# A decoder layer on one core: the feed-forward's first product as seven half-size products, its weight sums in a ring, and turned probabilities moved by half pairs

## Chip, cores and metric

The kernel runs on one core of a Trainium2 chip. The metric is the device time of one execution in microseconds. TensorE (PE) multiplies matrices, VectorE (DVE) and ScalarE (ACT) work element by element, GpSimd (POOL) does so too, and SyncE (SP) issues most of the DMAs. Each engine executes its instructions in the order in which the built program holds them.

## The reference

One decoder layer over 8 x 512 positions of width 512, with a layer norm behind each of its three parts. In the kernel `t` (0 to 7) is the first index and `j` a block of 128 of the 512 positions.

```python
x = layernorm(x + self_attn(x))          # 16 heads, over the 8 indices t, relative offsets
x = layernorm(x + cross_attn(ctx, x))    # 8 heads, 512 keys from a 512 x 1024 context, masked
x = layernorm(x + ffn(x))                # 512 -> 2048 -> 512

def ffn(x):
    h = relu(x @ w1.T + b1)              # float32
    hq = float_quantize(h, 4, 3)         # fp8
    return float_quantize(hq @ float_quantize(w2, 4, 3).T + bq, 5, 10)
```

The first product of `ffn` is, for each t, a 2048 x 512 matrix (w1) times a 512 x 512 matrix (x turned), in float32. It is what the change rewrites.

## The kernel before

The program has two phases.

**Phase 1** (to about 860 us) is the self-attention for each block j and, between its steps, the projection of the context into keys and values. For three pairs of t that projection is already done with seven half-size products in place of eight: sums of the weights (`sums_of_a`) and of the two contexts (`sums_of_b`) are formed on DVE, and each block of the result is a combination of a few products. The context sums stand in tiles `tx` (pool `tcp`, 4 buffers), read by the products `px` and `pz` (L662). A pacing planner written by hand (`must`, `fill`, `slot`) sets PE's order; the other engines' order in phase 1 is left to the scheduler. At the end of a block, `put_out` (from L346) multiplies the attention output by the output weights into the single bank of the pool `a_o`, loads the rows of x (`r`, L355, by SP), adds the bias to them on POOL (L356), adds the product on DVE (L362), and after every fourth t normalizes and stores the result to `x1d` (ACT's queue). In the last block, `put_out` for t = 4 to 7 is followed on PE by the context values of t = 6 (`psv`, L176).

**Phase 2** (from about 860 us) takes t = 0 to 7 in turn. All engines but POOL run in the order in which the steps are recorded. A function `weave` mixes two lists by their costs: the attention of t (scores `s`, weighted values `av`) and the "dense" steps. The dense steps of loop t are, in order: the output projection of t-1 (`project_x1`, `project_u`), its layer norm, the second feed-forward product of t-2 (`finish`, tile `o`), the queries of t+1 (`psq`, L1015), and the first feed-forward product of t-1 (`hidden`, tile `h`, L1229). Work on DVE, ACT and the queues that hangs on a step is put in lists (`urgent`, `side`, `moves`, `later`) and drained between the PE steps at a set pace.

- `hidden(t, n)` makes 128 of the 2048 rows at a time: four matmuls of 128 x 128 weights with the 512 positions of `x2T` moving, into one bank, then one ACT operation that adds the bias, applies relu and writes fp8 into `hq`. All of w1 (4 MB) lies in the buffer `big`, loaded once at t = 1.
- `x2T` is the layer norm's output in turned blocks: it is stored to `x2d`, loaded back in four DMAs (`load_blocks`, L937) and turned in place on DVE (`turn_x2`, L943), which stands between the queries 1 and 2 of the loop.
- The probabilities of one pair of heads, for a unit of half the queries (`jj` 0 or 1), are made by DVE and ACT in `scores`, turned in 32 x 32 blocks into `pb` (L1087), and, when both halves are there, moved across partitions into `pT` by 16 DMAs of 128 KB (`move_blocks`, L1102). All go to SP, but half of them to ACT's queue at t = 0. `pT` has one buffer, so the moves wait until `av` of the pair before has read it.
- At the end (after t = 7), `h` of the last t runs with nothing beside it but the second product of t = 6 and 7.

Of the kernel before, what the change touches and what calls it, by code (L numbers as in the profile page):

```python
# [17 lines left out]
P = 128  # L18
E = 512
# [23 lines left out]
def decoder_layer(  # L43
# [36 lines left out]
    def col(i):  # L80
        return colv[:, i : i + 1]
# [6 lines left out]
    x2d = [dram.tile([NJ, P, E], F32, name=f"x2d{t}") for t in range(T)]  # L88
    kd = [dram.tile([P, EC, S], F32, name=f"kd{t}") for t in range(T)]
    vd = [dram.tile([P, ST, E], F32, name=f"vd{t}") for t in range(T)]  # L90

    def load_row(pool, r, name):
        tl = pool.tile([P, E], F32, name=name)
# [38 lines left out]

    A11, A12, A22, S3, S1, S2, S4 = range(7)

    def sums_of_a(eng, w):
        eng.tensor_tensor(w[:, S1], w[:, S3], w[:, A22], ALU.add)
# [52 lines left out]
    with ExitStack() as ph:  # L191
# [570 lines left out]
        def last_but_one():  # L762
# [4 lines left out]
                T - 2, w6, lambda f: ct6[f], ps_kv, "kv", kst, "st"  # L767
            )

        filling.append(context_work())  # L770
        for j in range(NJ):
            for t in range(T) if j else range(2, T):
                if j and t == 0:
                    spare += [(FULL, values, j, u) for u in range(T)]
                items = []
                if t < T - 1:
                    items.append((FULL, queries_of, j, t + 1))


                if t < 4:  # L780
                    late = [t] if j or t > 2 else [0, 1, 2]
                else:
                    late = [[], [4, 5], [6], [7]][t - 4]
                items += [(0.9, offsets, j, u) for u in late]
                if j and t < 2:
                    items.insert(0, (0.9, turn_out, j - 1, T - 2 + t))
                if j and t < 3:
                    items.append((FULL, put_out, j - 1, T - 3 + t))
                slot(SCORES if j else SCORES + 1.9, items, T - 1 - t)
            softmax(j)  # L790
            last = j == NJ - 1
            if last:
                load_w6_keys()
                pieces = last_but_one()

                def values_in_turn():
                    load_w6_values()
                    yield -14.0
                    for piece in pieces[EC:]:
                        piece()  # L800
                        yield 2 * FULL

                filling.append(values_in_turn())
            else:
                spare += [(FULL, keys, j + 1, u) for u in range(T)]
            fill(clock + FULL)
            slot(SOFTMAX, [], max(len(spare) - 2, 0))
            for t in range(T):
                weigh(j, t)
                items = []  # L810
                if t > 1:
                    items.append((0.9, turn_out, j, t - 2))
                if t == T - 1:
                    if not last:
                        items.append((FULL, queries_of, j + 1, 0))
                if t > 2:
                    items.append((FULL, put_out, j, t - 3))
                if last and t == 0:
                    spare += [(2 * FULL, piece) for piece in pieces[:EC]]
                slot(VALUES, items, len(spare) if last else max(T - 3 - t, 0))  # L820
        for t in (T - 2, T - 1):
            must(0.9, turn_out, j, t)
# [25 lines left out]
    with ExitStack() as ph:  # L848
# [8 lines left out]
        mp = pool("mp", 1)  # L857
        kvd = pool("kvd", 2)
        sp = pool("sp", 7)
        pbp = pool("pb", 2)  # L860
        ptp = pool("ptp", 1)
        sm = pool("smb", 4)
        ps_b = pool("b_b", 4, space=PSUM)
# [50 lines left out]
        x1, x1T, qT, uT, mb, mvb, kT, v, pb, pT, x2T, hq, mvc = ({} for _ in range(13))  # L914

        def load(t):
            mbc = mp.tile([P, S], F32, tag="mbc", name=f"mbc{t}")
            nc.sync.dma_start(mbc, mask[t].partition_broadcast(P))


            mq = mp.tile([P, S], F32, tag="mq", name=f"mq{t}")
            nc.gpsimd.tensor_scalar(mq, mbc, -1.0 / math.sqrt(D2), None, ALU.mult)
            mb[t] = mp.tile([P, S], F32, tag="mb", bufs=2, name=f"mb{t}")
            nc.gpsimd.tensor_scalar(mb[t], mbc, 0.0, MASKED, ALU.is_equal, ALU.mult)
            qT[t] = qx.tile([P, EC, S], F32, tag="qT", bufs=2, name=f"qTx{t}")
            return mq

        def load_x1(t):
# [29 lines left out]
        def turn_x2(t):  # L958
            for c in range(EC):
                turn_in_place(x2T[t], c)  # L960

        def load_k(t, c):
            kT[t, c] = kvd.tile([P, S], F32, tag="kT", name=f"kT{t}_{c}")
# [48 lines left out]
        def queries(t, o, mq):  # L1012
            ps = bank(f"psq{t}_{o}")
            for e in range(EC):
                nc.tensor.matmul(  # L1015
                    ps,
                    lhsT=w_tgt[:, e, o * P : (o + 1) * P],
                    rhs=x1T[t][:, e, :],
                    start=(e == 0),
                    stop=(e == EC - 1),  # L1020
                )
            nc.vector.scalar_tensor_tensor(
                qT[t][:, o, :], ps, col(C_BT + o), mq, ALU.add, ALU.mult
            )

        def scores(t, c, jj):
# [4 lines left out]
            for j in js:  # L1031

                ps = ps_s.tile([P, 2, S], F32, tag="s", name=f"s{t}_{c}_{j}")
                for h in range(2):
                    nc.tensor.matmul(  # L1035
                        ps[:, h, :],
                        lhsT=qT[t][half[h], c, j * P : (j + 1) * P],
                        rhs=kT[t, c][half[h], :],
                        start=True,
                        stop=True,  # L1040
# [38 lines left out]
            def turn_blocks(i):  # L1079


                if i == 0 and jj == 0:
                    pb[t, c] = pbp.tile(
                        [P, 4, 2, ST, 2, 2, 32], F32, tag="pb", name=f"pb{t}_{c}"
                    )
                for h in range(2):
                    nc.vector.transpose(  # L1087
                        pb[t, c][:, :, jj, :, h, i, :].rearrange("p a k e -> p k a e"),
                        prs[2 * i + h].rearrange("p (k a e) -> p k a e", a=4, e=32),
                    )  # L1090

            def move_blocks():

                pT[t, c] = ptp.tile(
                    [P, 4, 2, ST, 2, 64], F32, tag="pT", name=f"pT{t}_{c}"
                )
                for i in range(4):
                    for a in range(4):
                        g = (a + i) % 4

                        queue = nc.scalar if t == 0 and a % 2 else nc.sync
                        queue.dma_start(  # L1102
                            pT[t, c][32 * a : 32 * a + 32, g],
                            pb[t, c][32 * g : 32 * g + 32, a].rearrange(
                                "p i k h j e -> p i k h (j e)"
                            ),
                        )

# [10 lines left out]
                side.append((u, 1.2, lambda i=i: divide(i)))  # L1119
            for i in range(2):  # L1120
                side.append((u, 1.3, lambda i=i: turn_blocks(i)))
            if jj == 1:
                side.append((u, 0.0, lambda: moves.append((u // 2, move_blocks))))

        def attend(t, c):

# [78 lines left out]
        def turn_last_x2(j):  # L1205
            t = T - 1
            if j == 0:
                settle(("x2", t))
                x2T[t] = qx.tile([P, EC, S], F32, tag="x2T", name=f"x2T{t}")
            turn(x2T[t], x1[t], j, f"x2tr{t}")  # L1210

        w1 = []

        def load_w1():

            w1.append(big.tile([P, EC, HID], F32, tag="big", name="w1"))
            for q in range(4):
                qs = slice(q * E, (q + 1) * E)
                nc.sync.dma_start(w1[0][:, :, qs], chunked(w1T)[:, :, qs])

        def hidden(t, n):

            if n == 0:

                tag, bufs = ("qT", 2) if t == T - 1 else ("hq", 1)
                hq[t] = qx.tile([P, HC, S], F8, tag=tag, bufs=bufs, name=f"hq{t}")
            ps = bank(f"h{t}_{n}")
            for e in range(EC):
                nc.tensor.matmul(  # L1229
                    ps,  # L1230
                    lhsT=w1[0][:, e, n * P : (n + 1) * P],
                    rhs=x2T[t][:, e, :],
                    start=(e == 0),
                    stop=(e == EC - 1),
                )
            nc.scalar.activation(  # L1236
                hq[t][:, n, :], ps, AF.Relu, bias=col(C_B1 + n), saturate=False
            )

        def finish(t, j, n):  # L1240

# [118 lines left out]
        with tc.manual_schedule(engines={ET.PE, ET.DVE, ET.Activation, ET.SP}):  # L1360
# [22 lines left out]
            scores(*units[0])  # L1383
            turn_v_soon(0)

            for t in range(T):

                pace = 1.3 if t == 0 else 0.7
# [29 lines left out]
                else:  # L1418
                    done = [of(3.8, finish, t - 2, j, NJ) for j in range(NJ) if t > 1]
                    if t == 1:  # L1420

                        done = [of(7.2, pieces[-2]), of(7.2, pieces[-1]), [], []]
                    dense += output_of(t - 1)
                    if t == 1:
                        dense[1:1] = of(0.0, convert, 2)
                    projected = len(dense)
# [10 lines left out]
                    if t == 1:  # L1437
                        dense += of(0.0, convert, 3)
                    if t == 1:
                        dense += of(0.0, load_w1)  # L1440
                    dense += done[2]
                    if t + 1 < T:
                        dense += of(0.0, turn_x1, t + 1)
                    dense += done[3]
                    dense += asked[:2] + of(0.0, turn_x2, t - 1) + asked[2:]
                    queried = len(dense)
                    for n in range(HC):
                        dense += of(3.6, hidden, t - 1, n)
                        if n == HC // 4:
                            dense += of(0.0, load_x1, t)  # L1450
                weave(dense, attention_of(t, projected, queried))

            last = of(3.8, finish, T - 2, 0, NJ) + output_of(T - 1)
            last += of(0.0, normalize_x2, T - 1)
            for j in (1, 2):
                last += of(3.8, finish, T - 2, j, NJ)
            for j in range(NJ):
                last += of(0.6, turn_last_x2, j)
            last += of(3.8, finish, T - 2, 3, NJ)
            for n in range(HC):  # L1460
                last += of(3.6, hidden, T - 1, n)
            for j in range(NJ):
                last += of(3.8, finish, T - 1, j, 1)
            for cost, step in last:
# [90 lines left out]
```

## Time and profile before

| | |
|---|---|
| runs | 2096.81, 2097.76, 2099.65 us; median 2097.76 |
| profiled execution | span 2097.7 us (its own time within 0.1 us of the median), granted PE clock 0.991 |
| PE busy | 2049.0 us (98%), 5768 records |
| DVE busy | 1432.4 us (68%) |
| ACT, POOL busy | 466.3 us (22%), 167.2 us (8%) |
| DMA | 255.27 MB, 122 GB/s mean |
| `h`, all of it | 451.8 us busy in 1024 records |
| moves `pT` from `pb` | 480 on SP's queue and 32 on ACT's, 128.0 KB each |

The profile is one execution, taken on the chip. A group of instructions is shown as line, engine, operation, output and inputs, shape and number, then its busy time, the mean duration of one, the engine's idle time just before them, and what ended that idle time. A float32 matmul leaves two records on PE. Matmuls are pipelined, so the mean duration of one is longer than the time from one start to the next. In a timeline a row is the start, the length, and the instructions that ran in it, with the idle time before in brackets. SPq rows are DMA issues: their length is what SP spends on issuing.

### The profile page before, as it was taken

Reading aid. Unit: us, or ns where it says so; the run is one execution under the profiler, and the core shown is the slowest. Engines: PE = TensorE matmul, PEld = TensorE weight load, DVE = VectorE, ACT = ScalarE, POOL = GpSimd, SP = SyncE. Lnnn points to the kernel's source line nnn. Section 1 sums busy time; section 2 is a strip of 40 time slices with the busy share of each in tenths; the row PEclk is TensorE's granted clock in tenths of the full one; section 3 lists DMA queues with packets and bytes.
Section 4 is the critical chain, followed back from the end, with each engine's and each line's share of the span. In section 5 each row is a group of like instructions: output and inputs, shape, how many; then the busy total and the mean of one; then the engine's idle time right before and its main releaser. Section 6 shows DMA issues by size and latency. Waiting matters only on the chain.

```text
span 2097.7 us, 17237 instructions
## 1 busy us (share of the span) xinstructions
PE 2049.0 (98%) x5768; PEld 889.9 (42%) x5768; DVE 1432.4 (68%) x2285; ACT 466.3 (22%) x955; POOL 167.2 (8%) x147
## 2 busy tenths in 40 slices
PE   9999999998999989998999999999999999999998
PEld 4544444444444434443443444444444434443443
DVE  4999999999899968367554754835747548357232
ACT  2111101110111101123232232231332322323211
POOL 0110120011001200121001011010010100001000
PEclk9999999999999989999999999999999999999999
DMA  6615333341131332885782744745636537437200
GB/s 217 225 40 201 106 105 131 110 155 65 57 144 60 137 149 70 260 222 139 160 214 67 133 118 101 136 116 93 139 84 110 141 87 146 100 80 152 53 21 20
DMA packets 246249, 255.27 MB, mean 122 GB/s; under 512 B 141072, under 2 KB 161552, under 8 KB 246160
## 3 DMA queue, kind: packets, MB, share of 16 engines
q1 hardware_dynamic: 227248, 219.25, 40.9%
q10 hardware_dynamic: 18912, 34.91, 5.0%
q8 instruction: 46, 0.75, 0.1%
q14 instruction: 43, 0.35, 0.1%
HBM read 130.36 MB, written 56.62 MB: 89 GB/s over the span
## 4 chain that ended last, share of the span: by engine, by line
PE 82%; DVE 13%; DMA 2%; issue 2%; SPq 0%; POOL 0%; ACT 0%; DVEq 0%; ACTq 0%
PE h L1229 21%; PE px L662 6%; PE s L1035 6%; PE pox L1174 5%; PE av L1137 5%; PE pox L1162 5%; PE psq L1015 5%; PE ps_k L216 5%; PE o L1246 4%; DVE pq L249 4%; DVE sc L258 3%; PE pz L662 3%; PE po L346 3%; PE psk L162 3%; PE psv L176 3%; PE ps_v L216 2%
## 5 line engine op out<-in xcount | busy, mean ns | idle before, releaser
L1229 PE MATMUL h<-x2T,w 128*128 128x512 f32 x1024 | 451.8, 596 | 2.3 <-DVE x2T L943 2.3
L1050 DVE CUSTOM_DVE_ANT_0 pe<-s,mb 128x512 f32<-128x512 f32 x256 | 162.1, 682 | 211.0 <-PE s L1035 211.0
L1229 PEld LDWEIGHTS h<-x2T,w 128*128 128x128 f32 x1024 | 191.1, 190 | 259.4 <-issue 254.2
L1060 ACT ACTIVATE pe<-pe,nmax 128x512 f32<-128x512 f32 x256 | 182.2, 712 | 209.1 <-DVE nmax L1050 178.9
L1087 DVE STREAM_TRANSPOSE pb<-pe 128x512 f32<-128x512 f32 x256 | 159.6, 679 | 0.0
L1236 ACT ACTIVATE hq<-h,colv 128x512 fp8e4<-128x512 f32 x128 | 87.9, 687 | 293.7 <-PE h L1229 293.7
L249 DVE TENSOR_TENSOR pq<-qw,k 128x2048 f32<-128x2048 f32 x64 | 151.1, 2361 | 1.1
L313 DVE TENSOR_TENSOR pv<-v,sc 128x2048 f32<-128x2048 f32 x64 | 146.5, 2290 | 1.9
L258 DVE TENSOR_REDUCE sc<-pq 128x64 f32<-128x2048 f32 x64 | 145.9, 2280 | 1.1
L1035 PE MATMUL s<-kT,qTx 64*128 64x512 f32 x512 | 127.2, 615 | 0.0
L216 PE MATMUL ps_k<-w_in,xt 128*128 128x512 f32 x256 | 118.0, 613 | 9.1 <-DMA xt<-in_xT_dram 4.9
L1137 PE MATMUL av<-pT,vx 128*64 128x512 f32 x512 | 118.5, 605 | 7.4 <-DMA mbc<-in_mask_dram 7.4
L216 PE MATMUL ps_v<-w_in,xt 128*128 128x512 f32 x256 | 116.4, 599 | 5.7 <-DVE qw L245 5.7
L346 PE MATMUL po<-w_o,aoT 128*128 128x512 f32 x256 | 115.5, 594 | 3.2 <-DVE r L362 3.2
L1075 DVE TENSOR_SCALAR pe<-pe,rden 128x512 f32<-128x512 f32 x256 | 114.9, 491 | 4.5
L216 PE MATMUL ps_q<-w_in,xt 128*128 128x512 f32 x256 | 116.0, 596 | 0.5 <-ACT v L286 0.3
L1174 PE MATMUL pox<-w_xo,uT 128*128 128x512 f32 x256 | 115.2, 598 | 0.0
L1162 PE MATMUL pox<-w_xo,x1Ts 128*128 128x512 f32 x256 | 114.4, 595 | 0.0
L1246 PE MATMUL o<-w2q,hq 128*128 128x512 fp8e4 x512 | 114.1, 379 | 0.0
L1015 PE MATMUL psq<-x1Ts,w_tgt 128*128 128x512 f32 x256 | 113.8, 597 | 0.0
L356 POOL TENSOR_TENSOR r<-r,bo 128x512 f32<-128x512 f32 x32 | 55.5, 1764 | 520.5 <-DMA r<-in_x_dram 323.9
L1181 DVE TENSOR_TENSOR x<-pox,x 128x512 f32<-128x512 f32 x32 | 22.1, 692 | 104.2 <-PE pox L1174 66.3
(142 smaller groups left out, 2150.1 us busy)
## 6 DMA issues: line engine op xcount, KB each, us to landing
pT<-pb SPq DMA_DIRECT2D x480, 128.0 KB, 2.4
ch<-in_ctxT_dram SPq DMA_DIRECT2D x24, 512.0 KB, 6.6
td<-tx SPq DMA_DIRECT2D x12, 768.0 KB, 4.8
tx<-td SPq DMA_DIRECT2D x12, 768.0 KB, 9.1
r<-in_x_dram SPq DMA_DIRECT2D x32, 256.0 KB, 3.4
x1d<-r ACTq DMA_DIRECT2D x32, 256.0 KB, 2.5
x1Ts<-x1d SPq DMA_DIRECT2D x32, 256.0 KB, 6.1
kT<-kd SPq DMA_DIRECT2D x32, 256.0 KB, 3.3
```

Of the source, the lines that this page charges most:

```text
L216: nc.tensor.matmul(ps, lhsT=xt[:, e, :], rhs=w_in[:, e, part * E : (part + 1) * E], start=(e == 0), stop=(e == EC - 1),)
L249: nc.vector.tensor_tensor(pr, qw[:, fs] .rearrange("p (h d) -> p h d", d=D1) .unsqueeze(2) .to_broadcast([P, HH, T, D1]), k_all[j][:, :, f ...
L258: nc.vector.tensor_reduce(sc[j][:, t, g * HH * T : (g + 1) * HH * T], pr.rearrange("p h s d -> p (h s) d"), AX.X, ALU.add,)
L662: nc.tensor.matmul(bank, lhsT=w7[:, a, f, i * P : (i + 1) * P], rhs=b[f], start=start and f == 0, stop=f == HF - 1, skip_group_check=not s ...
L1015: nc.tensor.matmul(ps, lhsT=w_tgt[:, e, o * P : (o + 1) * P], rhs=x1T[t][:, e, :], start=(e == 0), stop=(e == EC - 1),)
L1035: nc.tensor.matmul(ps[:, h, :], lhsT=qT[t][half[h], c, j * P : (j + 1) * P], rhs=kT[t, c][half[h], :], start=True, stop=True,)
L1060: nc.scalar.activation(pe, pe, AF.Exp, bias=nmax[:, h : h + 1], scale=-1.0, accum_out=den[:, h : h + 1],)
L1137: nc.tensor.matmul(av[half[h], :], lhsT=v[t, c][:, s, half[h]], rhs=pT[t, c][:, :, :, s, h].rearrange("p g i q -> p (g i) q"), start=(s == 0),
L1162: nc.tensor.matmul(po, lhsT=x1T[t][:, e, j * P : (j + 1) * P], rhs=w_xo[:, e, :], start=(e == 0), stop=False,)
L1174: nc.tensor.matmul(po, lhsT=uT[t][:, e, j * P : (j + 1) * P], rhs=w_xo[:, EC + e, :], start=False, stop=(e == EC - 1),)
L1229: nc.tensor.matmul(ps, lhsT=w1[0][:, e, n * P : (n + 1) * P], rhs=x2T[t][:, e, :], start=(e == 0), stop=(e == EC - 1),)
L1246: nc.tensor.matmul(po, lhsT=hq[t][:, c, j * P : (j + 1) * P], rhs=w2q[:, c, :], start=(c == 0), stop=(c == HC - 1),)
```

## The change

1. `hidden` is replaced by `hidden_of`. For each t the 2048 x 512 weights are taken as four groups, each of two halves of the rows (128 x 2 of the first half of the outputs, 128 x 2 of the second) and two halves of the contraction; the 512 positions are split in two halves of 256. A group needs seven products (`y`, `x1_`, `z`, `x2_`, `z2`, `x3`, `x4`) of four matmuls with 256 positions moving. Three of their results are copied with the bias by ACT (`keep`), three are added by DVE from PSUM (`add`) with a relu on ACT behind, and `x4` goes straight to relu. The last `x4` of a t is recorded in the next loop, behind its first `project_x1`.
2. The position sums: `sum_x2` records four additions on DVE behind the turn of `x2T`, between the queries 2 and 3.
3. The weight sums: `sum_w1` is recorded in the last eight slots of phase 1, twice in each. It takes a tile from `tx`'s buffers, loads four 128 x 128 blocks of w1, makes four additions on POOL and stores 7 x 128 columns to DRAM (`w1d`).
4. The weights, now 7/4 as large, don't stay: `big` holds a ring of two groups. Part 0 of a slot (three weights) is loaded again after `z`, part 1 (four weights) after `x4`, for the group after next.
5. `move_blocks` moves each half pair when it is turned: 16 DMAs of 64 KB per unit. `pb` has three buffers of a half pair in place of two of a pair.
6. The mask is loaded into its own tile `mq` without a tile `mbc`; the queries `qT` are four tiles per t with seven buffers; `hq` always has its own tag.

```diff
-    A11, A12, A22, S3, S1, S2, S4 = range(7)
+    A12, A11, S1, S2, S4, S3, A22 = range(7)
...
+        def sum_w1(n, f):
+            w = tcp.tile([P, 7, P], F32, tag="tx", name=f"w1s{n}_{f}")
+            for a, r, k in ((A11, 0, 0), (A12, 0, 1), (S3, 1, 0), (A22, 1, 1)):
+                o0 = r * (HID // 2) + n * P
+                nc.sync.dma_start(w[:, a], chunked(w1T)[:, 2 * k + f, o0 : o0 + P])
+            sums_of_a(nc.gpsimd, w)
+            nc.sync.dma_start(w1d[n // 2][:, :, f, (n % 2) * P : (n % 2 + 1) * P], w)
...
                     items.append((FULL, put_out, j, t - 3))
...
+                if last:
+                    for f in range(2):
+                        sum_w1(t, f)
                 slot(VALUES, items, len(spare) if last else max(T - 3 - t, 0))
...
+        def sum_x2(t):
+            b = blocks_of_x2(t)
+            x2s[t] = qx.tile([P, 3, 2, HALF], F32, tag="x2s", name=f"x2s{t}")
+            sums_of_b(
+                nc.vector,
+                b[0, 0],
+                b[0, 1],
+                b[1, 0],
+                b[1, 1],
+                *(x2s[t][:, i] for i in range(3)),
+            )
...
-            if jj == 1:
-                side.append((u, 0.0, lambda: moves.append((u // 2, move_blocks))))
+            side.append((u, 0.0, lambda: moves.append((u // 2, move_blocks))))
...
+            ps = slice(0, 3) if part == 0 else slice(3, 7)
+            nc.sync.dma_start(ring[0][:, q % 2, ps], w1d[q % GROUPS][:, ps])
...
+            def product(g, name, a, b, start):
+                w = ring[0][:, (t * GROUPS + g) % 2, a]
+                if start:
+                    banks[g, name] = bank(f"h{name}{t}_{g}").rearrange(
+                        "p (i q) -> p i q", i=2
+                    )
+                for f in range(2):
+                    for i in range(2):
+                        nc.tensor.matmul(
+                            banks[g, name][:, i],
+                            lhsT=w[:, f, i * P : (i + 1) * P],
+                            rhs=b[:, f],
+                            start=start and f + i == 0,
+                            stop=f == 1,
+                            skip_group_check=not (start and i == 0),
+                        )
+                return banks[g, name]
...
+            def keep(r, c, g, src):
+                st = kept[g, r, c] = hp.tile(
+                    [P, 2, HALF], F32, tag="hs", name=f"hs{t}_{g}_{r}{c}"
+                )
+                for i in range(2):
+                    nc.scalar.activation(
+                        st[:, i], src[:, i], AF.Identity, bias=bias(r, g, i)
+                    )
+
+            def add(r, c, g, src):
+                st = kept[g, r, c]
+                nc.vector.tensor_tensor(st, src, st, ALU.add)
+                nc.scalar.activation(target(r, c, g), st, AF.Relu, saturate=False)
...
+            def again(g, part):
+                later.append([1, lambda: load_w1(t * GROUPS + g + 2, part)])
...
+            def y(g):
+                start_of(g)
+                keep(0, 0, g, product(g, "y", A12, b(1, 0), True))
+
+            def x1_(g):
+                add(0, 0, g, product(g, "x", A11, b(0, 0), True))
+
+            def z(g):
+                keep(1, 1, g, product(g, "z", S1, x2s[t][:, 0], True))
+                again(g, 0)
+
+            def x2_(g):
+                keep(0, 1, g, product(g, "x", S2, x2s[t][:, 1], False))
+
+            def z2(g):
+                add(0, 1, g, product(g, "z", S4, b(1, 1), False))
+
+            def x3(g):
+                add(1, 1, g, product(g, "x", S3, b(0, 1), False))
...
+            order = [(y, 0), (x1_, 0), (z, 0)]
+            for g in range(GROUPS):
+                more = g + 1 < GROUPS
+                order += [(x2_, g), (z2, g)]
+                order += [(y, g + 1)] if more else []
+                order += [(x3, g)]
+                order += [(x1_, g + 1), (z, g + 1)] if more else []
+                order += [(x4, g)]
+            steps = [(1.8, lambda f=f, g=g: f(g)) for f, g in order]
+            return steps[:-1], steps[-1:]
...
-                    dense += asked[:2] + of(0.0, turn_x2, t - 1) + asked[2:]
+                    dense += asked[:2] + of(0.0, turn_x2, t - 1) + asked[2:3]
+                    dense += of(0.0, sum_x2, t - 1) + asked[3:]
```

## The prediction

> **What bounds the kernel now.** I read the busy table and the chain of waits first, then the groups, then the timelines of the stretches that the diff touches. The profiled execution's span is 2097.7 us; the median of the runs is 2097.76, so sums are made against 2097.7 and need no correction. Differences under 0.2% (4 us) count as no change.
>
> ```profile
> PE 2049.0 (98%) x5768; PEld 889.9 (42%) x5768; DVE 1432.4 (68%) x2285; ACT 466.3 (22%) x955; POOL 167.2 (8%) x147
> ...
> PE 82%; DVE 13%; DMA 2%; issue 2%; SPq 0%; POOL 0%; ACT 0%; DVEq 0%; ACTq 0%
> ...
> L1229 PE MATMUL h<-x2T,w 128*128 128x512 f32 x1024 | 451.8, 596 | 2.3 <-DVE x2T L943 2.3
> ```
>
> PE is the bound: 98% busy, 82% of the chain. A stretch with PE full, 1000 to 1900, has DVE at 524 of 900 us. The feed-forward's first product h is the largest PE group and waits only 2.3 us in all. An f32 matmul leaves two records, so its 512 instructions are x1024. Whatever makes PE wait is therefore added one for one, and whatever PE no longer does is gained one for one.
>
> **1. Fewer products: gain.** The chain of waits has the last position's h alone: 54.93 us for 128 records, 429 ns each. The new records are 128x256, which the trace lacks; the nearest are the bias products of phase 1, 128x128, 8 records in 1.05 us of a pipelined end, 16 in 1.95.
>
> ```profile
> 2022.38 54.93 PE h L1229 x128
> ```
>
> ```profile
> 648.59 1.05 PE L270 MATMUL bd<-gp,xt 128*128 128x128 f32 x8
> ...
> 700.90 1.95 PE L270 MATMUL bd<-gp,xt 128*128 128x128 f32 x16
> ```
>
> ```profile
> L270 PEld LDWEIGHTS bd<-gp,xt 128*128 128x128 f32 x256 | 33.5, 194 | 12.7 <-issue 12.7
> ```
>
> (1.95-1.05)/8 = 112 ns from start to start, with a new weight tile for every matmul, so weight loads of 194 ns overlap one another and don't bind at 112. A straight line between 112 (N=128) and 429 (N=512) gives 218 at N=256; ends are 214.5 (half of 429) and 224 (two of 112). New records: 8 positions x 4 groups x 7 products x 4 matmuls x 2 = 1792. 1792 x 0.218 = 390 against 1024 x 0.429 = 439: **-49 us** (-38 to -55).
>
> A rule speaks against this. The Trainium skill, "TensorE: Matmul & The Clock Gate", section "Back-to-back issue gap", says that in a stream with a weight load for every matmul the spacing is set by both, about 81 ns at N=128 where streaming alone gives 56. With 25 ns more per pass, by estimate from that page, a record would be some 268 ns and the change would lose 41 us here. Twice that page's unpenalised 56 is the 112 ns above, measured with weights that change every time, so this trace doesn't show the penalty.
>
> **2. Sums of the weights between the phases: loss.** The sums are recorded with the last slots of phase 1, but their tiles share the four buffers of the context sums tx, last read by the px products at 842.49. In the order of the built program, SP has r's load for put_out 4, then nearly all of the 64 loads of 64 KB and the 16 stores, and only then r's loads for 5 to 7; POOL has the 64 sums ahead of r's additions in the same way. PE works in order: put_out 6 needs the bank that DVE's addition of r for put_out 5 empties, and behind it stand put_out 7, the 64 records of psv and all of phase 2.
>
> ```profile
> 842.49 3.60 PE L662 MATMUL px<-tx,w 128*128 128x512 f32 x8
> 845.92 0.60 PE L337 MATMUL aot<-ident,ao 128*128 128x128 f32 x4
> 848.04 3.70 PE L346 MATMUL po<-w_o,aoT 128*128 128x512 f32 x8 [1.52 <-DVE r L362]
> 851.58 0.60 PE L337 MATMUL aot<-ident,ao 128*128 128x128 f32 x4
> 852.58 3.70 PE L346 MATMUL po<-w_o,aoT 128*128 128x512 f32 x8 [0.40 <-DVE r L362]
> 857.22 3.67 PE L346 MATMUL po<-w_o,aoT 128*128 128x512 f32 x8 [0.93 <-DVE r L362]
> 860.73 27.63 PE L176 MATMUL psv<-w6v,ct 128*128 128x512 f32 x64
> 888.19 7.03 PE L1015 MATMUL psq<-x1Ts,w_tgt 128*128 128x512 f32 x16
> ```
>
> ```profile
> 726.68 1.66 POOL L292 TENSOR_TENSOR sc<-sc,gc 128x128 f32<-128x128 f32 x4 [25.48 <-DVE sc L279]
> ```
>
> ```profile
> 1495.10 2.51 SPq L978 DMA_DIRECT2D raw<-vd  x4
> ```
>
> The first fence is PE's timeline, the others a softmax sum on POOL and four 64 KB loads on SP. Before the change POOL adds all four r from 845.63 (4 in 5.33 us), and DVE adds r for put_out 5 at 851.84. After: the first weight tile is free at 845.9. SP needs 0.49 to 0.63 us per 64 KB load (raw: 1.96 to 2.51 for four), so 64 loads and 16 stores at 0.37 are 37 to 46 us of issue. POOL, at four in 1.66 us, needs 27 us and is not the limit, but the stores wait for it and the buffers for the stores; a pair of tiles costs 5.9 to 7.2 us if landing (2.2), sums and stores are only half hidden. r's load for 5 then goes out at 883 to 901, +3.4 to land, +1.3 POOL, +0.7 DVE: 889 to 906 in place of 852.5. PE resumes 37 to 53 us late; value 46. After the 7.45 us gap at 983 the granted clock averages 0.66 over 990 to 996, worth 2 us, so I add 2. **+48 us**; bounds +26 (POOL alone limits) and +56. Nothing covers it.
>
> **3. Halves of the turned probabilities, and the ring, on SP: loss.** There are 1024 moves of 64 KB in place of 512 of 128 KB. One 128 KB move takes 0.63 us of SP (10.07 for 16); a 64 KB one should take 0.49 to 0.63 by the raw rows, so a position's 64 moves (40 us of SP) become 128 (63 to 81) of a period of 142 us. SP is idle enough on average; the damage is to what is queued behind a burst.
>
> ```profile
> 1471.16 5.38 SPq L937 DMA_DIRECT2D x2T<-x2d  x4
> 1482.85 10.07 SPq L1102 DMA_DIRECT2D pT<-pb  x16
> ```
>
> (a) Positions 1 to 5 of h (t=2..6): x2T's load now stands behind 16 half moves, so at 1478 to 1480 for 1471; its landing (9.5 us after the first issue) eats the 6 us that it had to spare before the turn at 1487.4, which ends at 1490 to 1492. From there DVE has 11.5 us of work in its order (exponentials, divisions and turns of one half pair, the last query's addition, four sums of x2 at 0.65, and the first addition, which reads the bank that the S2 product then adds to). PE, which has only 9 to 10 us of queries, scores and three products to do, waits: 0 to 5 us a position; value 2.4, sum 12.
> (b) Part 1 of the ring's third group (1.05 MB) is issued behind 32 moves, four raw loads, x1's 1 MB load and part 0 of the fourth group: 2.84 MB behind one another are 7 us at the 406 to 413 GB/s of the fullest windows of the trace (around 740 and 852), and with 16 to 20 us of issue for the moves they land 0 to 6 us after PE wants them; value 3. A wait in (a) gives (b) slack, so I count the larger, 3, plus half the other: for six positions **+21** together (0 to 65).
> (c) t=1: both halves of a pair, 32 moves, now stand before x2T's load (1050.77 today; h starts at 1067): **+10** (0 to 15).
> (d) t=0: av waits 7.45 us for pT at 983 today; 32 smaller moves on two queues: **+4** (-7 to +5).
> (e) t=7: h waits 2.28 us for x2T today, with DVE full: **+4** (0 to 8).
>
> **4. What costs nothing.** 96 additions and 32 sums of 0.69 us add 88 us to DVE, of which phase 2 has over 500 us idle; if that cover were gone in one loop, part (a) is where it shows. ACT's 128 outputs of 0.69 us become 96 whole and 256 half ones, 66 to 154 us more by half or the whole of that price, on an engine 351 of 1238 us busy after 860. Loading the mask into its own tile drops a buffer, no operation. In the tail, h alone becomes 224 records, 49 us for 55, contained in part 1; the ring's loads there have 8.6 us per group for 1.8 MB, about 7.4 with landing: 0 to 1 us.
>
> **Sum.** 2097.7 - 49 + 48 + 21 + 10 + 4 + 4 = 2135.7. The terms of part 3 are correlated, and a PE stall early in a position relieves the later ones; I take 6 us off: **2130 us**.
>
> **Rivals.**
> A (forecast, 0.56): wait between the phases and moderate waits in phase 2: 2106 to 2158.
> B (0.20): the wait between the phases is there, but phase 2's loads land in time: 2097.7 - 49 + 48 = 2097, 2085 to 2105. For it: x2T had 6 us of slack and SP is idle half the time. Against: the 32 moves ahead of the ring's load. Faster 0.09, same 0.08, slower 0.03.
> C (other side, 0.16): SP and POOL run through the sums fast enough. If loads issue at 0.32 us (SP's quickest rows) and stores don't block, r arrives by 878 and the loss is 26; with waits of at most 15 in phase 2, 2050 to 2090. It decides for faster as soon as boundary and phase 2 together cost under 45 us. For it: POOL needs only 27 us. Against: 64 KB loads at 0.49 and more.
> D (0.08): everything at its upper end, 2158 to 2185: 56 between the phases, 65 in (a) and (b).
> That the change doesn't do what it says (a record of 245 ns or more, 439/1792, so no gain at all) is inside A and D: 2150 to 2180; the 112 ns row speaks against it.
>
> **How the numbers follow.** Faster: C 0.16 + B 0.09 = 0.25. Same: 0.08 (B). Slower: A 0.56, D 0.08, B 0.03 = 0.67. The range 2066 to 2160 leaves out about half of C and D. If slower, the likeliest range alone is 2106 to 2158.
>
> **What would show it.** Step 1: h's records at 214 to 224 ns from start to start, 1792 of them. Step 2: PE idle some 40 to 50 us before a po product near 852, released by DVE's r, with POOL's weight sums and SP's loads filling 846 to 895, and psq at 925 to 940. Step 3: idle time before h's products, released by the ring's tile or by DVE's x2 sums, a few us at each position. I am wrong if psq starts before 915, or if h's idle time in phase 2 is near nothing; and if h's records are much above 224 ns.

## The result, and the profile after

The changed kernel takes 2256.94 us (median of 4 runs, 2254.2 to 2261.32) against 2097.86 for the kernel before on the same chips: a ratio of 1.0758, 95% interval 1.0743 to 1.0773. It is slower by 159 us, where 32 were forecast. The profiled execution's span is 2253.5 us, 155.8 longer than before; all sums below are made between the two spans.

The page of the changed kernel, busy times and the chain of waits:

```profile
PE 2036.6 (90%) x6536; PEld 1057.6 (47%) x6536; DVE 1515.7 (67%) x2413; ACT 543.8 (24%) x1179; POOL 195.4 (9%) x211
...
PE 63%; DVE 15%; DMA 10%; SPq 7%; issue 3%; ACT 1%; POOL 1%; ACTq 1%; DVEq 0%; POOLq 0%
```

PE is busy for 90% of the span and not 98%, and transfers (DMA) and SP's issuing (SPq) have 17% of the chain, where they had 2%. DVE and ACT are busier by 83 and 77 us, yet their share of the span has hardly moved. So PE now waits, and by the chain it waits for queues. PE's own waits (who waited <- what ended the wait: sum in us, number, longest):

```profile
PE po L348 <- DVE r L364: 60.9, 4, 58.1
PE hx L1279 <- DMA w1r<-w1d: 38.2, 7, 6.9
PE hx L1279 <- DVE hs L1307: 29.2, 7, 5.4
PE hy L1279 <- DMA w1r<-w1d: 19.7, 1, 19.7
PE hy L1279 <- DVE x2T L955: 12.4, 1, 12.4
PE s L1069 <- DVE nmax L1084: 11.2, 6, 4.1
...
PE av L1171 <- DMA raw<-vd: 6.8, 1, 6.8
```

One wait of 58 us stands between the phases (put_out); most others are at h, once or twice in every position. In the order of the rows: the S2 product (`x2_`, the product with the weight sum S2) of the third group, which waits for the ring; the S2 product of the first group, which waits for an addition; h's start at t = 1 and at t = 7. The last two rows are waits before scores, 1.3 to 4.1 us at t = 0, 2, 3 and 5, and before the first av of t = 0.

**Where the 156 us come from.** psq of t = 0 starts at 948.51, before at 888.19: **60 us** by the end of phase 1. Phase 2 from there takes 1305.0 us for 1209.5: 95.5 more. In it, PE's gaps of over 0.9 us sum to 118 us, before to 10: **+108**. The granted clock below 1 (busy time times what is missing, in stretches of 2 us) costs 34.7 us, before 1.6: **+33**. The products give back **52** (below). 108 + 33 - 52 = 89 of the 95.5; I have not followed the rest up.

**The products.** PE's timeline of the last position:

```profile
2183.27 1.89 PE L1279 MATMUL hy<-x2T,w1r 128*128 128x256 f32 x8
2185.00 1.89 PE L1279 MATMUL hx<-x2T,w1r 128*128 128x256 f32 x8
```

Eight records follow one another in 1.73 us, 216 ns each, with new weights every time: 1792 x 0.216 = 387 us against 439. The seven products do what they were meant to do.

**Between the phases.** PE's timeline, and SP's of one round of the weight sums:

```profile
909.79 6.31 PE L348 MATMUL po<-w_o,aoT 128*128 128x512 f32 x8 [58.12 <-DVE r L364]
917.03 3.67 PE L348 MATMUL po<-w_o,aoT 128*128 128x512 f32 x8 [0.93 <-DVE r L364]
...
948.51 14.00 PE L1048 MATMUL psq<-x1Ts,w_tgt 128*128 128x512 f32 x32 [0.34 <-DVE x1Ts L955]
```

```profile
865.08 0.52 SPq L778 DMA_DIRECT2D w1d<-w1s  x1
865.65 1.66 SPq L776 DMA_DIRECT2D w1s<-in_w1T_dram  x2
...
868.04 3.56 SPq L776 DMA_DIRECT2D w1s<-in_w1T_dram  x6
873.74 0.52 SPq L778 DMA_DIRECT2D w1d<-w1s  x1
...
904.11 0.38 SPq L357 DMA_DIRECT2D r<-in_x_dram  x1
```

A pair of tiles takes 8.0 to 8.7 us from one round to the next (here 865.08 to 873.74), and only after nearly all of them, at 904.11, does SP issue the row r that put_out 6 waits for. PE restarts at half its clock: 6.31 us for 8 records that take 3.67 in the next row.

**One position of phase 2.** SP, ACT and PE at t = 2:

```profile
1294.82 5.53 SPq L949 DMA_DIRECT2D x2T<-x2d  x4
...
1328.00 21.30 SPq L1137 DMA_DIRECT2D pT<-pb  x32
...
1351.96 0.92 SPq L1259 DMA_DIRECT2D w1r<-w1d  x2
```

```profile
1317.26 0.72 ACT L1094 ACTIVATE pe<-pe,nmax 128x512 f32<-128x512 f32 x1 [8.07 <-DVE nmax L1084]
...
1318.69 0.81 ACT L1301 ACTIVATE hs<-hy,colv 128x256 f32<-128x256 f32 x2
```

```profile
1320.28 3.78 PE L1279 MATMUL hx<-x2s,w1r 128*128 128x256 f32 x8 [5.37 <-DVE hs L1307]
1323.99 3.97 PE L1171 MATMUL av<-pT,vx 128*64 128x512 f32 x16
...
1361.72 3.75 PE L1279 MATMUL hx<-x2s,w1r 128*128 128x256 f32 x8 [6.89 <-DMA w1r<-w1d]
```

The first gap: the product y is done at 1311, but its copy on ACT runs at 1318.69. ACT had nothing to do for 8 us; it stood at an exponential whose maximum DVE had not made yet, and the copy is behind it in ACT's order. DVE's addition and then PE's S2 product follow. The second gap: av ends at 1327.96, 32 half moves then take SP 21.3 us (0.67 us each), and only behind them, four raw loads and x1's load come the ring's loads, which land 9 us after their issue. Behind both gaps the first 8 records take 3.75 and not 1.9 us.

### The profile page after: what moved, and what is told of

It reads as the page before. It is cut to its first block, busy times and chain, and to the rows that moved or that the text cites. A ratio compares the mean times of both kernels' runs of the same rounds, so it can differ in the third digit from the quotient of the medians.

```text
span 2253.5 us, 20114 instructions
## 1 busy us (share of the span) xinstructions
PE 2036.6 (90%) x6536; PEld 1057.6 (47%) x6536; DVE 1515.7 (67%) x2413; ACT 543.8 (24%) x1179; POOL 195.4 (9%) x211
## 4 chain that ended last, share of the span: by engine, by line
PE 63%; DVE 15%; DMA 10%; SPq 7%; issue 3%; ACT 1%; POOL 1%; ACTq 1%; DVEq 0%; POOLq 0%
PE hx L1279 9%; PE px L664 5%; PE pox L1196 5%; PE pox L1208 5%; PE ps_k L218 4%; SPq L1137 4%; PE av L1171 4%; PE hz L1279 4%; PE po L348 4%; PE s L1069 3%; PE pz L664 3%; PE ps_v L218 3%; PE ps_q L218 3%; DMA w1r<-w1d 3%; DVE pq L251 3%
## 5 line engine op out<-in xcount | busy, mean ns | idle before, releaser
L1279 PE MATMUL hx<-x2s,w1r 128*128 128x256 f32 x512 | 140.6, 430 | 67.5 <-DMA w1r<-w1d 38.2
L1307 DVE TENSOR_TENSOR hs<-hz,hs 128x512 f32<-128x512 f32 x32 | 22.1, 691 | 197.0 <-PE hz L1279 197.0
L1279 PEld LDWEIGHTS hx<-x2s,w1r 128*128 128x128 f32 x512 | 108.1, 215 | 95.0 <-issue 39.0
L1279 PE MATMUL hx<-x2T,w1r 128*128 128x256 f32 x512 | 118.1, 382 | 0.0
L1279 PEld LDWEIGHTS hx<-x2T,w1r 128*128 128x128 f32 x512 | 98.3, 192 | 14.0 <-issue 0.8
```

What stands on the lines that cost most here:

```text
L1279: nc.tensor.matmul(banks[g, name][:, i], lhsT=w[:, f, i * P : (i + 1) * P], rhs=b[:, f], start=start and f + i == 0, stop=f == 1, skip_gro ...
```

## The experiments

Two theories. **A, order:** the waits are made by what stands ahead in queues that are worked in order (SP, ACT, POOL), and go when that is moved. **B, load:** the added 66 MB, 83 us of DVE and 77 of ACT fill the engines, and waits come back wherever they are moved to. A kernel that was run once is compared by the span of that run (after: 2253.5; the four runs of the changed kernel have spans of 2252.5 to 2259.6, so differences under some 7 us say nothing).

**Weight sums made early**

```diff
-            w = tcp.tile([P, 7, P], F32, tag="tx", ...)
+            w = wsp.tile([P, 4, P], F32, tag="w1s", ...)   # pool of its own, 1 buffer
...
-                if last:
-                    for f in range(2): sum_w1(t, f)
+                if j == 2: sum_w1(t, 1)                    # and sum_w1(t, 0) in the SCORES slots
```

> Weight sums made during block 2 of phase 1, in a 2 KB tile of their own (four sums, and the unsummed weights copied from DRAM to DRAM), so that the rows r for put_out 5 to 7 stand behind nothing. Theory A (the loss lies in what stands ahead in the in-order queues): the 58 us idle before put_out 6 goes, with about 2 us of lowered clock after it; phase 2 is unchanged; about 2253 - 60 = 2193 us. Rival B (the sums cost by themselves, through GpSimd's and the DMA engines' load): they come back as DVE or DMA time in block 2, and less than half of the 60 us is won, 2223 or more.

Span 2231.7, 22 less. The 58 us wait is gone (no put_out waits longer than 1.5 us), and phase 2 is as it was, gap by gap. But put_out 7 starts at 896.5: phase 1 is 40 us longer than before, all of it before 390 us, in waits of 7.7 and 8.8 us and smaller ones at half clock. The tile waits for nothing, so the scheduler put its loads at the kernel's start, and SP, standing at them from 23.7 us on, issued the context's loads at 82.4 and not at 65.0. By its number the run lies in B's range (2223 or more), but not by its cause: the wait is cured as A says, and the price paid elsewhere is again one of order.

**x2T's load first**

```diff
-            while moves and moves[0][0] <= attended:
+            while moves and moves[0][0] <= attended and not held:
# held is set by normalize_x2 (t < 7) and cleared by load_x2T
```

> Moves of the turned probabilities are held back from the layer norm of x2 until x2T's load is issued, so that x2T's load stands ahead of the half moves on SP; nothing else changes. Theory A: x2T lands 8 to 10 us earlier at t = 2 to 6 and some 16 us earlier at t = 1; the waits before the S2 product (5.4 us, five times), before h at t = 1 (19.7) and t = 7 (12.4) mostly go, with the lowered clock after them: -40 to -65 us, 2190 to 2215. Rival B (DVE's order of work behind the turn, not the load, makes the waits): under -15 us, since the four sums and the first addition stay where they are in DVE's order.

Span 2229.3, 24 less, between the two. The S2 product's wait falls from 5.4 to 3.3 us at t = 2 to 5 and 2.3 at t = 6, not to nothing; h's waits at t = 1 (22.5) and t = 7 (12.1) stay. So x2T's lateness was less than half of that wait, and at t = 1 another one ends later: there the profile names the ring's first loads, as before.

**The ring's loads on ACT's queue**

```diff
-            nc.sync.dma_start(ring[0][:, q % 2, ps], w1d[q % GROUPS][:, ps])
+            nc.scalar.dma_start(ring[0][:, q % 2, ps], w1d[q % GROUPS][:, ps])
...
-                later.append([1, lambda: load_w1(t * GROUPS + g + 2, part)])
+                load_w1(t * GROUPS + g + 2, part)
```

> The ring's loads are issued on ACT's queue straight behind the product that frees their slot, not on SP behind the half moves; bytes, sizes and places are the same. Theory A (SP's queue makes part 1 late): the wait of 6 to 7 us before the third group's S2 product goes at every position, with some 2 us of lowered clock each: -45 to -60 us, 2195 to 2210. Rival B (bandwidth: the ring's 1.8 MB per group beside the other transfers cannot land in a group's 27 us): the waits stay at 4 us or more, since the loads land no faster; under -15 us.

Span 2235.4, 18 less. The ring's wait is gone at every t, so bandwidth is not its cause: the same bytes land in time when they are asked for in time. But h's wait at t = 1 grows to 29.3, av waits 9.0 at t = 7, and new waits of 2.5 us for ACT come in. The sign of A was right, its size was not: PE's waits in one loop are not independent.

**The three together**

> The three edits together: early sums, x2T's load first, ring on ACT's queue. Theory A: the three waits are separate places and their gains add up, 2253 - 60 - 50 - 50 = 2093, between 2060 and 2110, so what remains is the 49 us saved on products against what stays of phase 2's waits. Rival B (load): waits move to other places, 2150 or more.

2216.75 us (2211.71 to 2219.8), 1.056 of the kernel before (1.0536 to 1.0584). The three alone won 64 us of span, together 38. That is B's range. What is left: h at t = 1 (21.0) and 7 (13.1), the S2 product at 3.3, and now av, 20.5 us in all, for the half moves. This spoke for B, or for a cause that none of the three had touched: the half moves.

**Whole moves again.** The two halves of a pair are moved together, in 16 DMAs of 128 KB.

```diff
-        pbp = pool("pb", 3)                 # half pairs
+        pbp = pool("pb", 2)                 # whole pairs
...
-            side.append((u, 0.0, lambda: moves.append((u // 2, move_blocks))))
+            if jj == 1:
+                side.append((u, 0.0, lambda: moves.append((u // 2, move_blocks))))
...
-                st = kept[g, r, c] = hp.tile([P, 2, HALF], F32, tag="hs", ...)
+                st = kept[g, r, c] = hs[0][:, used[0] % 2]   # end of the ring's tile
+                used[0] += 1
```

In this kernel and in the second one with everything together, the slot of the copy kept for the quarter (1, 1) is taken by the next group's first copy before it is added, so that quarter's values are those of another product; the instructions and their sizes are the same.

> Part 5 alone undone: turned probabilities move as whole pairs again (16 DMAs of 128 KB per pair); to make room, the kept products lie in two slots in the unused end of the ring's tile and the queries have six buffers. The ring, its bytes and SP's queue for it stay. Theory A (half moves, each taking as much of SP as a whole one, make the ring's part 1 and x2T late): the wait before the third group's S2 product falls from 6 or 7 us to under 2, h's wait at t = 1 from 19.7 to under 5 and at t = 7 from 12.4 to under 5; the S2 wait behind the hidden start falls only to about 3.3, as with x2T's load first: 2253 - 85 = 2165, between 2145 and 2185. Rival B (the ring's bytes are the cause): part 1's wait stays at 4 us or more and the total above 2215.

Span 2159.2, 94 less: the forecast within 6 us, though h's waits at t = 1 and t = 7 stay above the 5 us forecast for them. Of PE's waits at h, this is left, and 5.7 us at t = 7:

```profile
PE hx L1281 <- DVE w1r L1308: 18.9, 7, 3.3
...
PE hy L1281 <- DMA w1r<-w1d: 9.9, 1, 9.9
```

No wait for the ring is left but its first load, with the ring's 58.7 MB still loaded by SP. The burst before its load is 16 moves of 0.70 us (11.21 for 16) in place of 32 of 0.67. A half move costs SP what a whole one does (0.59 us is the median of one issue for both); that is what made the loads behind it late. The run also has other slots for the kept products, six query buffers and the wrong quarter; the pair of runs further down, with right values, gives 91 us for the same exchange. The lowered clock in phase 2 falls from 34.7 us to 17.1.

**The first products of h without side work**

```diff
-            steps = [(1.8, lambda f=f, g=g: f(g)) for f, g in order]
+            steps = [(0.0 if i < 3 else 2.0, ...) for i, (f, g) in enumerate(order)]
```

> The first three products of h (y, x1, z of group 0) are recorded at no cost in the pacing, so that no exponentials, divisions or turns are put ahead of their copies and additions on ACT and DVE; nothing else changes. Theory A (the 5.4 us before the S2 product is a wait for the copy of y on ACT, behind exponentials that wait for DVE): that wait falls to under 2 us at t = 2 to 6, with some of the lowered clock: -20 to -35 us, 2218 to 2233. Rival B (DVE is simply late because x2T lands late, or the work put off makes PE wait at the next scores): less than 10 us won.

Span 2259.9: nothing won, which is B's number though not its reason. The mechanism of A was right and the gain was not: the S2 product's wait falls from 5.4 to 2.3 us, and the ring's wait grows from 6 or 7 to some 10.7, 67.5 us in all.

```profile
PE hx L1279 <- DMA w1r<-w1d: 67.5, 7, 11.1
...
PE hx L1279 <- DVE hs L1307: 10.6, 6, 2.3
```

The changed costs also put av behind more products of h; the moves cannot start before av has ended, and the ring's loads stand behind the moves. An earlier wait taken away was given back at the later one.

**Weight sums in the middle of phase 1**, in r's four buffers, four tiles behind each four put_outs of blocks 1 and 2:

```diff
+            w = rp.tile([P, 4, P], F32, tag="r", ...)
...
+                if j in (1, 2) and t == 6: sum_four(2 * j - 2)    # behind put_out 3
...
+                if j in (2, 3) and t == 2: sum_four(2 * j - 3)    # behind put_out 7
```

> The weight sums in r's buffers, four tiles behind each group of four put_outs from block 1 on, so that they can neither run at the start of the kernel (which took the context's and x's loads 40 us back in the run with early sums) nor stand ahead of the last rows r. Theory A: the 58 us before put_out 6 goes and phase 1 stays within 5 us of its length, about 2253 - 60 = 2193, 2185 to 2200. Rival B (the sums cost phase 1 in GpSimd, SP or DMA time wherever they are): phase 1 ends 20 us or more later than 842, 2213 or more.

Span 2207.3, 46 less: the 58 us are gone, but put_out waits 13.9 and 11.1 us twice, where the next r had to wait for the four tiles behind put_out 3. Behind put_out 7, where the next r is 100 us away, no wait appears. The same four tiles cost 11 to 14 us in one place and none in the other.

**Everything together, second version:** whole moves, these sums, h's first products without side work, the ring on ACT's queue.

> Everything together: whole moves, weight sums in mid phase 1, the first products of h without side work, and the ring's loads on ACT's queue. Theory A: no wait in phase 2 of over 3 us but the first av at t = 0, so the 49 us of products are mostly won: 2055 to 2085, faster than the kernel before. Rival B (88 us more on DVE, more on ACT and 66 MB more to move always find a place to stop PE): 2100 or more.

2099.15 us (2096.44 to 2107.41), ratio 1.0005 (0.9991 to 1.0018): level with the kernel before, between the two forecasts. From t = 2 to 6 PE has no gap of over 0.9 us. What is left are the two waits in phase 1 (13.9 and 10.7), 7.1 us before the first av, 20.1 us at t = 1 (x2T again behind 16 moves), and 5.7 and 2.7 at t = 7.

**Half moves alone, in the kernel before**

> The kernel before with part 5 of the change alone: half moves of 64 KB (1024 in place of 512) and three half buffers; h, its weights and all else as before. Theory A (half moves put work ahead of x2T's load on SP): x2T has 6 us to spare there, so h waits some 8 to 15 us at t = 1 and little at t = 2 to 6, with lowered clock after it: +8 to +30 us, 2106 to 2128. Rival B (half moves hurt only together with the ring's loads): within 4 us of the kernel before.

2121.47 us (2118.56 to 2122.06), 1.0104 of before (1.0089 to 1.0119), inside A's forecast; B is out.

```profile
PE h L1229 <- DMA w<-in_w1T_dram: 7.7, 1, 7.7
```

Most of the 23 us are at t = 0 and 1: phase 1 ends 2 us later, the scores of t = 0 wait 1.8 and 3.3 us, h of the first position starts 19 us later, with a wait of 7.7 for w1 behind 16 moves and x2T's load, and from there to h of t = 7 the two kernels differ by 3 us. So half moves cost 23 us without the ring, and 94 with it.

**Everything, mended**, and the same **with half moves**. The sums stand behind put_out 7 of blocks 0 and 1 only, x2T's load goes first, and the copies have free slots.

```diff
-                if j in (1, 2) and t == 6: sum_four(2 * j - 2)
-                if j in (2, 3) and t == 2: sum_four(2 * j - 3)
+                if j in (1, 2) and t == 2: sum_four(2 * j - 2); sum_four(2 * j - 1)
...
-                st = kept[g, r, c] = hs[0][:, used[0] % 2]
+                st = kept[g, r, c] = hs[0][:, r & c]
```

> The run with everything together, mended in three places: the weight sums stand only behind put_out 7 of blocks 0 and 1, where the next r is 100 us away; the moves of the turned probabilities are held until x2T's load is issued (it stood behind 16 moves at t = 1, 20 us of waiting); and each kept product has a slot that is free when it is written. Theory A: the 14 and 11 us in phase 1 and most of the 20 us at t = 1 go, with their lowered clock: 2097 - 45 = 2052, 2043 to 2065. Rival B: the waits move, 2080 or more.

2107.64 us (2103.49 to 2111.39), ratio 1.0042 (1.0026 to 1.0058): a miss, and in B's range. h's wait at t = 1 falls from 20 to 11.7, but eight tiles in a row now stand before the context's loads of the next pair:

```profile
PE py L664 <- DMA ch<-in_ctxT_dram: 36.4, 7, 13.2
PE hy L1296 <- DMA pT<-pb: 17.4, 2, 11.7
```

From put_out 7 to the end it takes 1213.5 us, before 1240.5: phase 2 has won 27, and phase 1 has lost 31.

> As the mended run with everything, but with half moves as in the change (and the kept products in their own pool, seven query buffers). Theory A: 32 moves of 0.6 to 0.9 us for one pair keep SP busy for over 20 us, so av waits 3 to 4 us at t = 2 to 6 and some 9 at t = 7, with lowered clock: 30 to 50 us above the run with whole moves, 2080 to 2110. Rival B (once x2T's load and the ring no longer stand behind them, half moves are free or help): within 10 us of the run with whole moves.

2198.54 us (2185.94 to 2201.41), 1.0462 of before (1.0422 to 1.0502): 91 us above the run with whole moves, twice what A forecast, and of the same size as the 94 us won in the change itself.

```profile
PE av L1184 <- DMA pT<-pb: 45.6, 12, 8.2
...
PE hy L1294 <- DVE x2T L967: 21.1, 1, 21.1
```

With the ring's loads on another queue and x2T's load ahead of them, half moves are late for av itself, twice a position.

**Sums spread over blocks 2 and 3,** four tiles behind the slots t = 2 and t = 5, all else as in the mended run.

> The mended run with everything, its weight sums moved once more: four tiles each in two places of blocks 2 and 3 of phase 1, in none of which the context's loads for the next pair or rows r are due (in blocks 0 and 1 eight tiles in a row held the context's loads up, 11 and 13 us of waiting). Theory A (the sums cost only what waits behind them in a queue, and phase 2 is 27 us shorter than before): phase 1 back to within 6 us of before and the whole 2066 to 2082, faster than the kernel before. Rival B (the sums' own traffic and GpSimd time lengthen phase 1 wherever they stand): 2090 or more.

2092.18 us (2089.1 to 2095.84), ratio 0.9968 (0.9956 to 0.9981): 0.3% faster than the kernel before, by 6 us and not by the 16 to 32 forecast; the number lies in B's range (2090 or more). Phase 1 still ends 16 us late:

```profile
PE px L664 <- DVE st L706: 18.1, 3, 13.1
```

One px product waits 13.1 us at 747, in the block where eight of the tiles stand. Its trace shows the queue:

```profile
744.14 1.22 DVE L297 TENSOR_REDUCE mx<-sc 128x128 f32<-128x1024 f32 x1 [12.40 <-POOL sc L294]
```

```profile
741.23 1.26 POOL L358 TENSOR_TENSOR r<-r,bo 128x512 f32<-128x512 f32 x1 [4.10 <-DMA r<-in_x_dram]
```

DVE's addition for px stands behind the softmax maximum (`mx`), which waits 12.4 us for POOL's product `sc`. POOL makes weight sums until 737.1, then waits 4.1 us for a row r that SP issued at 737.58, behind the tiles' last store, adds it, and only then makes `sc`; before the change DVE waits 1.2 us there. So this cost too is one of order, as A says, on POOL and SP. Whether a place without any cost is to be found, where the 24 to 27 us won in phase 2 would show in full, stays open.

## Why the prediction was wrong

The sign was right and so were most places named; the sum was 127 us short (124 between the spans), and the time fell outside the range. Of the 124, the waits of steps 3a and 3b make 46 (67 us for 21), the lowered clock in phase 2 makes 33, step 2 makes 12, 3c 10, 3e 6, 3d 2, waits before scores at t = 2, 3 and 5, which I did not name, 5, and the 6 us taken off for relief 6; step 1 gave 3 more than assumed, and some 6 us I have not followed up.

- **Step 1 (-49):** 216 ns for the 218 assumed, -52 us. The rule from the Trainium skill, "TensorE: Matmul & The Clock Gate", section "Back-to-back issue gap", by which pairs of weight load and short matmul would be slower, is not what this trace shows, with new weights for every matmul: the measurement decides.
- **Step 2 (+48, upper end 56):** the mechanism is the one predicted, at the very instruction, but it cost 60. Mis-sized is the pair of tiles, 8.1 us for 5.9 to 7.2. SP's issue alone (eight loads at 0.65 and two stores at 0.53, not 0.37) is 6.3; SP then stands 1.4 to 2.1 us at a store for its sums, and POOL stands some 4.2 us of every round at loads that SP issues only behind that store. Issue, landing and sums follow one another more than I assumed: I had let half of them overlap.
- **Step 3b (ring, 3 us a position):** 4.6 to 6.9 us measured. The half moves took the upper end of my price or more, 0.63 to 0.67 us, 20.1 to 21.3 for 32; the burst starts when av ends, 27 us before PE wants the weights, and burst, four raw loads and a landing of 9 us make 34. The run with whole moves shows that the moves, and not the bytes, were the cause: no wait for the ring is left from t = 2 to 6.
- **Step 3a (S2, 2.4 us a position):** 5.2 to 5.4 measured, and half of the reason was wrong. I counted DVE's work behind the turn. x2T's load gives 2.1 of the 5.4 (the run with its load first); the copy of y behind exponentials in ACT's order, which I did not look at, is what the addition waited for at t = 2, and side work gives 3.1 (the run without it, which takes work off DVE and ACT alike).
- **"A wait in (a) gives (b) slack":** this failed. Both waits were there in full. The moves start at the end of av, which stands behind (a), so (a) pushes the moves and the ring's loads back with it. An early wait moved the later one here and did not pay for it; counting only half of (a), and taking 6 us off for the same reason, both failed.
- **Step 3c (t = 1, 10):** 19.7. Behind x2T came the ring's first four loads, 3.6 MB behind the same 32 moves; I priced x2T alone. **3e (t = 7, 4):** 12.4, of which whole moves take away 6.7. **3d (t = 0, +4):** the gaps of t = 0 are 13.8 us for 7.45, +6. The size was nearly right, but not the place: av waits 6.8 us, less than before, and the other 7.0 us stand before scores, which wait for kT and for the maxima of DVE.
- **The clock, the largest omission.** I added 2 us for one gap. But I had put one or two gaps into most positions, and the trace of before has a lowered clock behind shorter gaps too: 0.57 in the 4 us from 731 and from 506, behind gaps of 2.8 and 4.1 us (1.00 behind the 2.3 us at 1906). There were some 15 such gaps, and they cost 33 us more in phase 2: as much as the whole forecast loss.
- **Rivals:** B (phase 2's loads land in time) and C (r arrives by 878) are both refuted by the first timelines; D came closest and was 72 us short; it too had only one lowered clock, which is 33 of them. Step 4 stands as far as load goes: added DVE and ACT time costs nothing by itself (ACT's order is what cost, in 3a); with the queues put in order, PE has no gap over 0.9 us from t = 2 to 6.

## What to carry to other kernels

Price an added transfer by what stands behind it in its queue, not by its bytes: 58.7 MB of ring loads left no wait from t = 2 to 6 once 16 whole moves, and not 32 half ones, stood ahead of them. When a DMA is cut in half and its issue time is not, count the burst twice and see who is next. And where PE is full, a new gap can have two prices, its length and the time at a lowered clock after it (some 2 us each here); multiply the second by the number of gaps.

## What the runs showed of the hardware

- One issue of a 64 KB move of 32 partitions took SP 0.59 us (median of 960 in the changed kernel), and one of a 128 KB move 0.59 us (median of 480 before); in unbroken bursts both take 0.63 to 0.73 us each. Halving a move saved the queue nothing. Landing is 2.0 us for 2.4.
- After most gaps the granted clock was 0.50 for some microseconds. The rows of the changed kernel around the first gap of t = 2, windows with PE's busy time first and the clock third from the end:

```profile
1315.00:1320.00 5.00, 0.00 (x0) 0.00 (x0) 3.86 (x10) 2.74 (x7) 0.00 (x0) 0.78 0.81 205
1320.00:1324.00 4.00, 3.72 (x10) 2.51 (x10) 3.93 (x12) 2.35 (x7) 0.00 (x0) 0.50 0.32 133
```

  In all runs, 8 records of 128x256 behind a gap took 1.97 to 1.99 us after gaps of 1.5 to 1.8 us, anything from 1.99 to 3.78 after 1.9 to 4.0, and 3.46 to 3.78 after 4.5 to 7. The Trainium skill, "TensorE: Matmul & The Clock Gate", section "What's actually happening", puts the drop at an idle window of about 3.4 us that runs freely; here 1.9 us were at times enough (2.93 us for the 8 records behind a gap of 1.95 at t = 7 of the changed kernel).
